# Linear attention in chunks of 64 instead of 128, with the small products in two shared PSUM banks

## The chip, the core and the metric

The kernel runs on one core of a Trainium2 chip. The metric is the device time of one execution in microseconds. A core has a matrix engine (TensorE, "PE" in the profile; its weight loads are listed as "PEld"), a vector engine (VectorE, "DVE"), a scalar engine for activations and copies (ScalarE, "ACT"), a general one (GpSimd, "POOL") and a queue for transfers (SyncE, "SP"). Each engine works through its own list of instructions in order; semaphores hold an instruction until those of other engines that it needs are done. TensorE writes its results to PSUM, which has eight banks of 512 fp32 values in each of 128 partitions; VectorE and ScalarE read them there.

## The reference

One block of a transformer in fp32: 4 sequences of 2048 tokens, 256 features. First linear attention with a running state over 16 heads of 16 features, then a mixture of 8 experts of which each token takes two, both behind a layer norm that is scaled and shifted per sequence.

```python
mod = (silu(c) @ wmod).reshape(4, 6, 1, 256)
sa, ca, ga, sb, cb, gb = (mod[:, i] for i in range(6))   # ga, gb kept away from 0
h = layernorm(x) * (1 + ca) + sa
x = x + ga * attention(h)
h = layernorm(x) * (1 + cb) + sb
x = x + gb * experts(h)

# attention: q = phi(h Wq), k = phi(h Wk), v = h Wv, phi = elu + 1, per head
S = S + k[:, None] * v[None, :]        # token by token
z = z + k
out = (S^T q) / max(z . q, 1e-6)       # then times w_out

# experts: top 2 of softmax(h w_router), at most 1280 tokens per expert in token order;
# y = sum over the two of gate * (silu(h w_gate) @ w_down[e])
```

## The kernel before

The 8192 tokens are 16 groups of 512 (`G`), a group is four steps of 128 tokens, and a sequence is four groups. A program of two halves: the attention half (to about 605 us of the span) goes through the 64 steps, and writes the rows of the expert stage to a DRAM array by indirect transfers; the expert half reads them in blocks and adds its results to the output.

In the attention half the order of TensorE, ScalarE, VectorE and GpSimd is the order in which the code names the instructions. While step `s` (group `g`, step `j` of it, counted from 0) attends, the same loop works on other groups: the queries, keys, values and denominators of group `g + 1` (`nxt`), the layer norm and keys of `g + 2` (`nrm`), the row sums of `g + 3` (`far`), the second norm, router logits and ranks of `g - 1` (`prv`), the slots and the sending of rows of `g - 2` (`old`). `early` is group 14, `tail` group 15 and the closing step.

Attention over a chunk of 128 tokens, for all heads at once in strips of 32 partitions (`a`) and two halves (`h`):

- `scores` (L494) multiplies keys and queries into `psc`, 4 banks, and VectorE masks them to the causal triangle in two instructions (L500) into `at`.
- `from_state` (L557) multiplies the state before the chunk with the scaled queries `qs` into the bank `po`; `attend` (L570) adds the masked scores times the values. `from_state` of a step is issued at the end of its turn, `attend` in the next turn.
- `keep_state` (L514) multiplies the chunk's keys and values into other columns of `po`. `take_out` (L525) copies both out on ScalarE; GpSimd adds the new part to the state and masks it (L538, L540).
- `project_out` (L588) multiplies the result with the output weights into a bank `pw`; VectorE adds it to the residual `x` (L589) and takes its statistics (L325).

Around it, per group: `project` (L375; `exk`, `exq` and relu on ScalarE, L379 and L380; the final product on VectorE, L384 and L389), `running_keys` (scan L433 on VectorE, product `qs` L438 on GpSimd), `denominators` (`pd` L446, `den` L451, `rden` L453), `scaled_q` (`pr` L464, `qs` L471), `heads_apart` (`qeo` L484 on ScalarE), `keys_by_token` (transposes L417), `values` (L397, copied to `vpad` L405), `sums`, squares in `deviations` and `normalise` (ScalarE, L282, L309, L348), `to_features` (L361, `hTa` and `hTm` L362). The router: `logits` (`pl` L640, `lgT` L645), `logits_by_token` (`lt` L653), `ranks` (L669 to L699, with one exp on ScalarE, L672), `positions` (`pp` L707 and L708, `pos` L712), `dispatch` (13 small products and an integer cast on VectorE, L731 to L753), `scale_rows` (GpSimd, L612), `shift_rows` (VectorE, L618), `send` (L770, the indirect transfers on GpSimd's queue).

PSUM: three banks `ps` that turn over among all products (`bank`), four for `psc`, one for `po`. The framework orders accesses of different engines to the same tile in PSUM by semaphores.

Of the kernel before, what the change touches and what calls it, by code (L numbers as in the profile page):

```python
# [40 lines left out]
P = 128  # L42
# [7 lines left out]
NT = G // P  # L50
GPB = L // G
# [7 lines left out]
SLOTS = NE * CAP  # L59
O_GB, O_CW, O_TOK, W = D, 2 * D, 2 * D + NE, 2 * D + NE + 4  # L60
# [7 lines left out]
def adaln_block(ctx: ExitStack, tc, x, wqkvT, woutT, wrT, wgT, wdT, cT, wmod, out):  # L68
# [4 lines left out]
    ps = ctx.enter_context(tc.tile_pool(name="ps", bufs=3, space=PSUM))  # L73
# [16 lines left out]
    tri = const.tile([P, P], F32, name="tri")  # L90
    bd = const.tile([P, 2, DH], F32, name="bd")
# [24 lines left out]
    ps_o = tokens.enter_context(tc.tile_pool(name="ps_o", bufs=1, space=PSUM))  # L116
    w1 = tokens.enter_context(tc.tile_pool(name="w1", bufs=1))
# [35 lines left out]
    def constants_last():  # L153
        make_upper_triangular(nc, tri, 1.0, diag=True)
        nc.gpsimd.tensor_copy(bd, par.unsqueeze(2).to_broadcast([P, 2, DH]))
# [61 lines left out]
    def row_products(i, pair):  # L217
        pg = bank(f"pg_{i}")
        for n, m in enumerate(pair):
            for k in range(NH):  # L220
                nc.tensor.matmul(
                    pg[:NB, n * D : (n + 1) * D], sc[:, k, :], wmod_sb[:, k, m * D : (m + 1) * D],
                    start=(k == 0), stop=(k == NH - 1),
                )
        return pg
# [71 lines left out]

    def deviations(m, a):

        nm = G_.pop("nm")  # L300
# [4 lines left out]
        if a is not None:  # L305
            xn = G_["xna", a]
            sq = small.tile([P, NT], F32, tag="sqa", name=f"sqa_{a}")
            for j in range(NT):
                nc.scalar.activation(  # L309
                    xn[:, j, :], xs[a][:, j, :], AF.Square, bias=nm[:, NT + j : NT + j + 1],  # L310
                    accum_out=sq[:, j : j + 1],
                )
            nc.gpsimd.tensor_scalar(ve[:, NT:], sq, 1.0 / D, LN_EPS, ALU.mult, ALU.add)
# [126 lines left out]
    def denominators(g):  # L440

        zq = G_["qs", g]
        pd = bank(f"pd_{g}")
        for h in range(NH):
            for j in range(NT):
                nc.tensor.matmul(  # L446
                    pd[32 * j : 32 * j + 32, :P], hpick[:, h, :], zq[:, h, j * P : (j + 1) * P],
# [3 lines left out]
        nc.vector.tensor_scalar(den, pd[:, :P], DEN_EPS, None, ALU.max)  # L451
# [5 lines left out]
    def scaled_q(g):  # L457
# [3 lines left out]
        pr = ps_sc.tile([P, 4, NH, 2, P], F32, tag="psc", name=f"pr_{g}")  # L461
        for h in range(NH):
            for j in range(NT):
                nc.tensor.matmul(  # L464
                    pr[:, j, h, 0, :],
# [4 lines left out]
        for h in range(NH):  # L470
            nc.vector.tensor_tensor(  # L471
                qs[:, h, :].rearrange("p (j t) -> p j t", t=P), qT[:, h, :].rearrange("p (j t) -> p j t", t=P),
                pr[:, :, h, 0, :], ALU.mult,
# [13 lines left out]
    def scores(g, j):  # L487
        kT, qeo = G_["k", g], G_["qeo", g]
        cols = slice(j * P, (j + 1) * P)
        psc = ps_sc.tile([P, 4, NH, 2, P], F32, tag="psc", name=f"psc_{g}_{j}")  # L490
        for h in range(NH):
            for a in range(4):
                r = 32 * a
                nc.tensor.matmul(  # L494
                    psc[:, a, h], kT[r : r + 32, h, cols], qeo[r : r + 32, h, :, cols],
                    start=True, stop=True,
                )
        for m in range(2):
            at = w4.tile([P, 2 * NH * 2, P], F32, tag="at", name=f"at_{g}_{j}_{m}")
            masked = nc.vector.tensor_tensor(  # L500
                at,
                psc[:, 2 * m : 2 * m + 2].rearrange("p i h q t -> p (i h q) t"),
                tri.unsqueeze(1).to_broadcast([P, 2 * NH * 2, P]),
                ALU.mult,
            )
            G_["at", g, j, m] = at.rearrange("p (i h q) t -> p i h q t", i=2, h=NH)
        return masked

    def keep_state(g, j):

        both, vp = G_["po"], vpads[g % 2]
        for h in range(NH):
            for a in range(4):
                nc.tensor.matmul(  # L514
                    both[32 * a : 32 * a + 32, D + 32 * h : D + 32 * h + 32],
                    G_["kk", g][:, j, h, 32 * a : 32 * a + 32], vp[:, j, h * 4 + a, 0::2, :],
                    start=True, stop=True,
                )

    def take_out(last, g, j):  # L520

        lo = 0 if last is not None else D
        hi = D + 32 * NH if g is not None else D
        both = w2.tile([P, D + 32 * NH], F32, tag="both", name=f"both_{g}_{j}")
        nc.scalar.copy(both[:, lo:hi], G_["po"][:, lo:hi])  # L525
        if last is not None:
            G_[("oT",) + last] = both[:, :D].rearrange("p (h t) -> p h t", h=NH)
        if g is None:
            return
        add = both[:, D:]  # L530
        if g % GPB == 0 and j == 0:
            G_["s_acc"] = add
        elif g % GPB == 0 and j == 1:
            s_acc = w1.tile([P, NH * 32], F32, tag="s_acc", name=f"s_acc_{g}")
            nc.gpsimd.tensor_tensor(s_acc, G_["s_acc"], add, ALU.add)
            G_["s_acc"] = s_acc
        else:
            nc.gpsimd.tensor_tensor(G_["s_acc"], G_["s_acc"], add, ALU.add)  # L538
        s_msk = w2.tile([P, NH, 2, DH], F32, tag="s_msk", name=f"s_msk_{g}_{j}")
        nc.gpsimd.tensor_tensor(  # L540
            s_msk, G_["s_acc"].rearrange("p (h q e) -> p h q e", h=NH, q=2),
# [599 lines left out]
```

## Time and profile before

| | before |
|---|---|
| median of 9 runs | 913.71 us |
| lowest, highest | 910.29, 918.58 us |
| the profiled execution, time | 917.34 us |
| its span, first to last instruction | 915.4 us |
| mean granted TensorE clock | 0.957 |
| busy: PE, DVE, ACT, POOL | 826.9, 567.9, 419.0, 476.7 us |
| scores, masks (L494, L500) | 74.5 us of 1024 records, 150.1 us of 128 |
| attend, from state, keep (L570, L557, L514) | 69.9, 40.8, 18.1 us |

The durations below come from this one profiled execution. The profile counts a TensorE instruction twice (an fp32 matmul is two records of 2 x 128 columns and the like), and records that run side by side in different strips overlap, so that busy time and mean durations of the narrow products say little; from the start of one block to the start of the next is what they cost. An "idle before" in brackets names the engine and line whose end ended the wait.

### The profile page before, as it was taken

To read this page: it belongs to the slowest core of one execution; us is meant where nothing else is said; L and a number is where in the kernel's file an instruction comes from. 1 tells how busy PE (TensorE), PEld (TensorE's weight loads), DVE (VectorE), ACT (ScalarE), POOL (GpSimd) and SP (SyncE) were. 2 spreads that over 40 slices of the span, in tenths; PEclk is the share of its full clock that TensorE was granted. 3 is DMA by queue.
4 is the path that set the end of the run, shared out by engine and by line. 5 is a ranking of instruction groups with operands and counts; after the bars stand their busy time and mean duration, and the time that the engine had idled before them with its cause. 6 is when DMAs were issued, how large, how long until landed. Compare 5 with 4: busy or idle time off the path is not lost.

```text
span 915.4 us, 20612 instructions
## 1 busy us (share of the span) xinstructions
PE 826.9 (90%) x8245; PEld 577.5 (63%) x8245; DVE 567.9 (62%) x1158; ACT 419.0 (46%) x972; POOL 476.7 (52%) x605
## 2 busy tenths in 40 slices
PE   6899989999999899999999977539999999999995
PEld 3476657657567567667657655336776767767764
DVE  3666788988888888988888885513333333333331
ACT  3557757666566566576667413212222222222220
POOL 2333356675576576576667576523443444434334
PEclk9999999999999999999999988659999999999998
DMA  8399862342442242232122111155665656545233
GB/s 291 112 360 347 214 138 70 106 141 68 120 137 97 75 142 88 95 111 86 52 76 63 41 53 35 58 200 140 146 140 106 133 109 148 109 102 111 35 34 41
DMA packets 75111, 108.25 MB, mean 118 GB/s; under 512 B 9578, under 2 KB 47218, under 8 KB 75016
## 3 DMA queue, kind: packets, MB, share of 16 engines
q1 hardware_dynamic: 47672, 68.91, 24.7%
q0 software_dynamic: 21760, 31.99, 16.1%
q10 hardware_dynamic: 5584, 6.04, 2.0%
q8 instruction: 65, 1.06, 0.5%
q14 instruction: 30, 0.25, 0.1%
HBM read 45.07 MB, written 74.69 MB: 131 GB/s over the span
## 4 chain that ended last, share of the span: by engine, by line
PE 66%; DVE 15%; issue 6%; POOL 5%; ACT 4%; DMA 2%; POOLq 0%; DVEq 0%; ACTq 0%; SPq 0%
PE ph L821 14%; PE pe L834 13%; PE pq L375 6%; PE pv L397 5%; PE psc L494 5%; PE pk L375 5%; PE po L570 5%; PE pw L588 4%; DVE at L500 3%; PE po L557 3%; DVE sel L751 2%; DVE qs L471 2%; POOL slots L770 2%; PE pte L810 2%; ACT hrow L348 2%
## 5 line engine op out<-in xcount | busy, mean ns | idle before, releaser
L843 POOL DMA_INDIRECT out_dram<-y,tok x80 | 123.3, 1541 | 180.8 <-DVE y L839 126.8
L500 DVE TENSOR_TENSOR at<-psc,tri 128x1024 f32<-128x1024 f32 x128 | 150.1, 1214 | 30.2 <-PE psc L494 29.9
L770 POOL DMA_INDIRECT slots<-hrow,idx x128 | 129.2, 1009 | 53.8 <-issue 38.7
L821 PE MATMUL ph<-hTe,wg_sb 128*128 128x512 f32 (+1 forms) x384 | 153.5, 527 | 0.0
L834 PE MATMUL pe<-wd,hid 128*128 128x256 f32 x640 | 150.5, 379 | 0.0
L827 DVE SCALAR_TENSOR_TENSOR hid<-th,ph 128x512 f32<-128x512 f32 (+1 forms) x96 | 57.5, 599 | 146.4 <-ACT th L826 146.4
L834 PEld LDWEIGHTS pe<-wd,hid 128*128 128x128 f32 x640 | 121.6, 190 | 37.0 <-issue 23.0
L826 ACT ACTIVATE th<-ph 128x512 f32<-128x512 f32 (+1 forms) x96 | 50.5, 526 | 156.4 <-PE ph L821 156.4
L821 PEld LDWEIGHTS ph<-hTe,wg_sb 128*128 128x128 f32 x384 | 70.3, 193 | 39.0 <-issue 32.5
L375 PE MATMUL pk<-hTa,wqkv_sb 128*128 128x512 f32 x128 | 70.4, 680 | 22.8 <-DVE gates L671 22.7
L494 PE MATMUL psc<-qeo,k 32*128 32x256 f32 x1024 | 74.5, 405 | 2.4 <-DVE qs L471 1.0
L588 PE MATMUL pw<-wob,both 128*128 128x256 f32 x236 | 63.3, 391 | 7.8 <-ACT both L525 5.5
L570 PE MATMUL po<-at,vpad 128*32 128x128 f32 x2048 | 69.9, 278 | 0.0
L839 DVE SCALAR_TENSOR_TENSOR y<-pe,rows 128x256 f32<-128x256 f32 x80 | 38.7, 484 | 49.6 <-PE pe L834 49.6
L570 PEld LDWEIGHTS po<-at,vpad 128*32 128x32 f32 x2048 | 53.9, 111 | 17.1 <-issue 17.0
L375 PE MATMUL pq<-hTa,wqkv_sb 128*128 128x512 f32 x128 | 61.3, 603 | 0.0
L494 PEld LDWEIGHTS psc<-qeo,k 32*128 32x128 f32 x1024 | 47.7, 187 | 19.7 <-issue 13.4
L397 PE MATMUL pv<-wqkv_sb,hTa 128*128 128x256 f32 x256 | 59.2, 384 | 0.0
L588 PEld LDWEIGHTS pw<-wob,both 128*128 128x128 f32 x236 | 41.8, 192 | 25.1 <-issue 10.1
L813 ACT COPY hTe<-pte 128x512 f32<-128x512 f32 (+1 forms) x48 | 24.7, 514 | 70.9 <-PE pte L810 70.8
L375 PEld LDWEIGHTS pk<-hTa,wqkv_sb 128*128 128x128 f32 x128 | 23.8, 203 | 47.6 <-issue 46.0
L397 PEld LDWEIGHTS pv<-wqkv_sb,hTa 128*128 128x128 f32 x256 | 47.6, 190 | 6.5 <-issue 0.4
(166 smaller groups left out, 1351.6 us busy)
## 6 DMA issues: line engine op xcount, KB each, us to landing
slots<-free SPq DMA_DIRECT2D x80, 262.0 KB, 4.9
rows<-slots SPq DMA_DIRECT2D x16, 1048.0 KB, 6.3
x<-in_x_dram SPq DMA_DIRECT2D x16, 512.0 KB, 5.9
out_dram<-x SPq DMA_DIRECT2D x16, 512.0 KB, 2.9
hrow<-mod_d SPq DMA_DIRECT2D x48, 128.0 KB, 3.6
rows<-slots SPq DMA_DIRECT2D x8, 524.0 KB, 4.6
wd<-in_wdT_dram ACTq DMA_DIRECT2D x8, 512.0 KB, 4.7
slots<-hrow,idx POOLq DMA_INDIRECT x128, 2.9
```

The lines of the kernel that those rows point to most:

```text
L375: nc.tensor.matmul(pq, wqkv_sb[:, k, o + h * P : o + (h + 1) * P], hT[:, k, :], start=(k == 0), stop=(k == NH - 1))
L397: nc.tensor.matmul(pv[:, i * D : (i + 1) * D], hT[:, k, (j + i) * P : (j + i + 1) * P], wqkv_sb[:, k, 2 * D : 3 * D], start=(k == 0), stop ...
L494: nc.tensor.matmul(psc[:, a, h], kT[r : r + 32, h, cols], qeo[r : r + 32, h, :, cols], start=True, stop=True,)
L500: masked = nc.vector.tensor_tensor(at, psc[:, 2 * m : 2 * m + 2].rearrange("p i h q t -> p (i h q) t"), tri.unsqueeze(1).to_broadcast([P, ...
L570: nc.tensor.matmul(po[32 * a : 32 * a + 32, h * P : (h + 1) * P], vp[:, j, h * 4 + a, q : q + 2, :], att[a // 2][:, a % 2, h, q, :], start ...
L588: nc.tensor.matmul(pw[:, :D], oT[:, h, :], wob[:, h, :], start=(h == 0), stop=(h == NH - 1))
L770: row = nc.gpsimd.indirect_dma_start(out=slots[:, :], out_offset=bass.IndirectOffsetOnAxis(ap=idx[:, c, j : j + 1], axis=0), in_=hr[:, j0 ...
L821: nc.tensor.matmul(ph[:, :m], wg_sb[:, k, f * P : (f + 1) * P], hTs[b][:, k, :m], start=(k == 0), stop=(k == NH - 1),)
L826: nc.scalar.activation(th[:, :m], ph[:, :m], AF.Tanh, scale=0.5)
L827: nc.vector.scalar_tensor_tensor(hids[b][:, f, :m], th[:, :m], 1.0, ph[:, :m], ALU.add, ALU.mult)
L834: nc.tensor.matmul(pe[:, :D], hids[b][:, f, j * P : (j + 1) * P], wds[e][:, f, :], start=(f == 0), stop=(f == NF - 1),)
L843: put = nc.gpsimd.indirect_dma_start(out=out[:, :], out_offset=bass.IndirectOffsetOnAxis(ap=toks[b][:, j : j + 1], axis=0), in_=y, in_offs ...
```

## The change

Attention works on two chunks of 64 tokens within a step. `scores` computes the two 64x64 diagonal blocks instead of one of 128x128, and one mask instruction covers all four strips. `po` is now one tile of two banks, allocated once, bank `c` for chunk `c`; the state is carried over twice per step, so `from_state` is issued for chunk 0 at the end of the turn and for chunk 1 in the next turn, ahead of `attend`. `take_out` copies the result on ScalarE; the new state is masked by VectorE straight out of PSUM (`new`) and added by GpSimd. The small products `pd`, `pw`, `pl`, `lt`, `pp` and `pg` move to free columns of `po`, and `ps` shrinks to two banks, which hold projections, transposes and values and are read by ScalarE (in the last group and the setup some small ones stay there). The order around it changes: squares and sums are issued ahead of `take_out`, the second norm too; `shift_rows` moves from step 1 to step 0, `dispatch` from step 2 to step 1, `send` of a group begins in step 2 instead of step 3.

```diff
-    ps = ctx.enter_context(tc.tile_pool(name="ps", bufs=3, space=PSUM))
+    ps = ctx.enter_context(tc.tile_pool(name="ps", bufs=2, space=PSUM))
...
+    po = ps_o.tile([P, 2, 512], F32, tag="po", name="po")
...
+    def squares(a):
+        xn, nm = G_["xna", a], G_["nm"]
+        sq = G_["sq", a] = small.tile([P, NT], F32, tag="sqa", name=f"sqa_{a}")
+        for j in range(NT):
+            nc.scalar.activation(
+                xn[:, j, :], xs[a][:, j, :], AF.Square, bias=nm[:, NT + j : NT + j + 1],
+                accum_out=sq[:, j : j + 1],
+            )
...
-        pd = bank(f"pd_{g}")
+        pd = po[:, 0, O_SMALL : O_SMALL + P]
...
     def scores(g, j):
+        psc = ps_sc.tile([P, 4, 512], F32, tag="psc", name=f"psc_{g}_{j}")
+        hq = psc[:, :, : NH * 2 * C].rearrange("p a (h q t) -> p a h q t", h=NH, q=2)
+        for h in range(NH):
+            for c in range(2):
+                cols = slice(j * P + c * C, j * P + (c + 1) * C)
+                for a in range(4):
+                    r = 32 * a
+                    nc.tensor.matmul(
+                        hq[c * C : (c + 1) * C, a, h], kT[r : r + 32, h, cols], qeo[r : r + 32, h, :, cols],
+                        start=True, stop=True,
+                    )
+        at = w4.tile([P, 4, NH * 2, C], F32, tag="at", name=f"at_{g}_{j}")
+        masked = nc.vector.tensor_tensor(
+            at,
+            psc[:, :, : NH * 2 * C].rearrange("p a (n t) -> p a n t", t=C),
+            tri_c.unsqueeze(1).unsqueeze(1).to_broadcast([P, 4, NH * 2, C]),
+            ALU.mult,
+        )
...
+    def keep_state(g, j, cs):
+        vp = vpads[g % 2]
         for h in range(NH):
             for a in range(4):
+                for c in cs:
+                    rows_ = slice(c * C, (c + 1) * C)
+                    o = NH * C + h * 32
+                    nc.tensor.matmul(
+                        po[32 * a : 32 * a + 32, c, o : o + 32],
+                        G_["kk", g][rows_, j, h, 32 * a : 32 * a + 32], vp[rows_, j, h * 4 + a, 0::2, :],
+                        start=True, stop=True,
+                    )
+
+    def take_out(last, g, j, cs):
+        n, o, k = NH * 32, NH * C, len(cs)
         if last is not None:
+            oT = G_[("oT",) + last] = w2.tile([P, NH, 2, C], F32, tag="oT", name=f"oT_{g}_{j}")
+            nc.scalar.copy(
+                oT.rearrange("p h c t -> p c h t"), po[:, :, :o].rearrange("p c (h t) -> p c h t", t=C)
+            )
...
+        st = w2.tile([P, 2, n], F32, tag="st", name=f"st_{g}_{j}", bufs=3)
+        new = st if first else w2.tile([P, 2, n], F32, tag="new", name=f"new_{g}_{j}")
+        nc.vector.tensor_tensor(
+            new[:, :k].rearrange("p c (h q e) -> p c h q e", h=NH, q=2),
+            po[:, :k, o : o + n].rearrange("p c (h q e) -> p c h q e", h=NH, q=2),
+            bd.unsqueeze(1).unsqueeze(1).to_broadcast([P, k, NH, 2, DH]), ALU.mult,
+        )
+        if not first:
+            nc.gpsimd.tensor_tensor(st[:, 0], G_["state"], new[:, 0], ALU.add)
+        if k == 2:
+            nc.gpsimd.tensor_tensor(st[:, 1], st[:, 0], new[:, 1], ALU.add)
...
     def project_out(g, j):
-        pw = bank(f"pw_{g}_{j}")
+        pw = po[:, 1, O_SMALL : O_SMALL + D]
...
-    def logits_by_token(part):
+    def logits_by_token(part, beside=False):
-        lt = G_["lt", part] = bank(f"lt_{g}_{j0}")
+        lt = G_["lt", part] = po[:, 0, O_SMALL : O_SMALL + P] if beside else bank(f"lt_{g}_{j0}")
...
+            if prv is not None and j == 2 and not early:
+                second_norm(prv)
+            if not tail and j == 0 and s > 0 and nrm is not None:
+                squares(nrm)
+            if not tail and j == 3 and far is not None:
+                sums(far)
             if last is not None:
+                from_state(*last, 1)
                 attend(*last)
...
+            keep_state(g, j, cs)
+            if prv is not None and j == (2 if early else 3):
+                logits(prv, beside=True)
+            if old is not None and j == 1:
+                positions(old, beside=True)
+            take_out(last, g, j, cs)
...
-            if old is not None and j == 3 and not early:
-                send(old, 0, 3)
+            if old is not None and j in (2, 3) and not early:
+                send(old, 3 * (j - 2), 3 * (j - 1))
...
             if g < NG:
-                from_state(g, j)
-                G_["s_old"] = G_.get("s_new")
+                from_state(g, j, 0)
+                G_["state"] = G_["next"]
```

`from_state` and `attend` change in the same way as `keep_state`: an inner loop over the chunks, 64 partitions and 64 columns where there were 128.

## The prediction

> **What bounds the kernel now.** I read the page's chain first: where does the time lie that set the end? Two thirds on TensorE.
>
> ```profile
> span 915.4 us, 20612 instructions
> PE 66%; DVE 15%; issue 6%; POOL 5%; ACT 4%; DMA 2%; POOLq 0%; DVEq 0%; ACTq 0%; SPq 0%
> ```
>
> The expert half (from 605 us) is not touched. The attention half is 16 groups of four steps, mostly 33 to 35 us each, so I read one steady group in the timeline (start, duration, engine, line). TensorE:
>
> ```profile
> 335.25 1.03 PE L588 MATMUL pw<-wob,both 128*128 128x256 f32 x4
> 338.18 1.96 PE L375 MATMUL pk<-hTa,wqkv_sb 128*128 128x512 f32 x4 [1.91 <-DVE gates L671]
> 340.06 0.64 PE L557 MATMUL po<-qs,s_msk 32*32 32x128 f32 x16
> 340.63 1.15 PE L494 MATMUL psc<-qeo,k 32*128 32x256 f32 x16
> ...
> 345.53 1.88 PE L375 MATMUL pq<-hTa,wqkv_sb 128*128 128x512 f32 x4
> 347.34 0.64 PE L557 MATMUL po<-qs,s_msk 32*32 32x128 f32 x16
> 347.91 1.15 PE L494 MATMUL psc<-qeo,k 32*128 32x256 f32 x16
> 348.98 1.08 PE L570 MATMUL po<-at,vpad 128*32 128x128 f32 x32
> 349.88 0.31 PE L514 MATMUL po<-vpad,kk 128*32 128x32 f32 x16
> 350.12 1.09 PE L417 MATMUL pk<-ident,k 128*128 128x128 f32 x8
> ```
>
> Start to start, a step's attention costs 0.57 (from the state) + 1.07 (scores) + 0.90 (attend) + 0.24 (keep) = 2.78 us. TensorE has one hole per group, 1.91 us before the second key projection, whose bank the router's logits hold until VectorE has read them. VectorE in the same group:
>
> ```profile
> 341.25 0.41 DVE L589 TENSOR_TENSOR x<-x,pw 128x256 f32<-128x256 f32 x1
> 348.56 0.69 DVE L384 SCALAR_TENSOR_TENSOR q<-exq,q 128x512 f32<-128x512 f32 x1 [0.77 <-ACT q L380]
> 349.17 1.28 DVE L433 TENSOR_TENSOR_SCAN zc<-ones_g,zc,k 128x512 f32<-128x512 f32 x1
> 350.37 2.33 DVE L500 TENSOR_TENSOR at<-psc,tri 128x1024 f32<-128x1024 f32 x2
> 355.04 1.27 DVE L618 TENSOR_TENSOR hrow<-hrow,modr 128x1024 f32<-128x1024 f32 x1
> 365.83 2.02 DVE L751 SCALAR_TENSOR_TENSOR sel<-rank,slot 128x32 f32<-128x32 f32 x1
> ```
>
> VectorE runs late and it costs nothing: the residual add of step 3 (341.25) ends 11 us after that step's scores began (330.67), and no TensorE work stands behind it, since its bank rotates. A 32-element product takes 2.02 us where it mostly takes 0.19: GpSimd's 2.37 us product ran from 365.43 to 367.80.
>
> Last, the granted clock in two stretches (columns after the five engines: clock, DMA share, GB/s):
>
> ```profile
> 232.00:267.00 35.00, 32.95 (x447) 22.18 (x446) 29.08 (x57) 22.00 (x54) 22.58 (x33) 0.95 0.35 119
> 335.00:368.00 33.00, 30.93 (x446) 21.81 (x445) 28.81 (x57) 21.62 (x54) 21.97 (x32) 1.00 0.34 116
> ```
>
> In the first the projection after the hole took 3.50 us instead of 1.96. In the chain it takes 3.02, 3.50, 3.41 and 3.42 in four of the twelve groups with that hole: the clock fell, at a cost of 1.4 us on average.
>
> **Part by part: the work.** A block's time is about 0.1 us of switching, a first weight load, and packs of strips that run side by side: a pack of four takes 0.109 us where 128 columns stream (eight packs in attend, four in state), 0.03 us for 32. Halved chunks double the instructions and halve the streamed columns, with twice the strips. If eight run side by side: scores 4 x 0.109 + 0.16 = 0.60; attend 8 x 0.055 + 0.13 = 0.57; state 4 x 0.055 + 0.13 = 0.35, now twice; keep 0.24 to 0.36, I take 0.30. Sum 2.17, so 0.6 us less per step, 38 us over 64 steps if TensorE set the time. If only four run side by side, scores stay at 1.03 and attend at 1.0, and a step costs 3.0: both ends are kept.
>
> VectorE drops 64 of 128 masks (1.21 us each, 78 us) and gains 64 products of 128x128 out of PSUM (row of den, 0.28 us: 18 us). ScalarE's copy goes from 320 to 256 columns; GpSimd trades a masking for a second add (0.5 us each). These count only where something waits.
>
> **The waits.** All small results now lie in the one tile po. The built program lists what each instruction waits for, and po is held whole: ScalarE's copy of oT comes before VectorE's product "new"; pw (L588's successor) waits for new, in step 2 for den, in step 3 for the read of the logits (steps counted from 0); and the next step's state products wait for the residual add. So each step makes a round trip PE, ACT, DVE, PE. I follow a group from mark to mark.
>
> *P (end of the second query projection, 347.34) to V (end of values, 355.91): 8.57 before.* VectorE is through the scan at 350.37, P + 3.03. The shift of rows has moved here (1.20), then one mask (1.13) and new (0.30): P + 5.66. TensorE reaches pw at P + 3.4 (0.35 + 0.60 + 0.35 + 0.57 + 0.30, positions 0.36, transposes 0.93). A hole of 2.3 us where there was none. V = 5.75 + pw 0.87 + values 3.63 = 10.25, so +1.7.
>
> *V to S3 (scores of step 3, 363.74): 7.83 before.* ScalarE copies vpad until V + 0.64, normalises four rows (2.0, now ahead of the oT copy), copies (0.36): V + 3.0; new until V + 3.35. Then pd 0.56, den, pw, rden 0.95, pr 0.68, transposes 1.0, qs: S3 at V + 7.55, with two holes of 0.4. That is -0.3. But the 13 small products of dispatch now stand before this step's mask, and start while GpSimd multiplies qs (1.27 us). One of them may be held, as sel was: 0 to 1.0 on this path; I take 0.5. Net +0.2.
>
> *S3 to S0 (scores of the next group, 340.63): 9.95 before.* ScalarE: hTm ends at S3 + 0.7, sums 1.6 (now ahead), lgT and oT until S3 + 3.05. Then, in its order, two qeo (1.3), exk and relu of the first keys (0.95), two qeo (1.3), and only then the exp of the gates: S3 + 6.8. From there VectorE needs 2.92 us to the residual add in the trace (338.33 to 341.25), + 0.41: S3 + 10.15. TensorE has finished both key projections at S3 + 7.7. The old hole of 1.91 goes (0.7 before pw is left); a hole of 2.5 before the state products takes its place. S0 = 10.25 + 0.35 = 10.6, so +0.65.
>
> *S0 to P: 6.71 before.* The squares, moved ahead of the oT copy (4 x 0.49), end before TensorE is through its first projection, which covers them. If it did not, pw would wait up to 1 us. Only here do the narrower tiles count: 0.60 + 0.35 + 0.57 + 0.24 + 4.5 = 6.25, so -0.45.
>
> Sum: +1.7 + 0.2 + 0.65 - 0.45 = +2.1 us per group. Groups 2 to 13 are like this: 12 x 2.1 = 25. Groups 0 and 1 lack the shift or the ranks, and group 14 and the last one (502 to 605 us) wait on GpSimd's sends and small chains; there the earlier sends (3 x 1.3 us out of group 14) and shorter masks stand against the new round trips: 0, between -6 and +6.
>
> The clock: two holes of 2.3 to 2.5 us per group instead of one of 1.9. If half of them are followed by a drop of 1.4 us: 1.4 - 0.33 x 1.4 = 0.9 per group, 11 us; bounds 0 and 12 x 2.3 = 28. [...]
>
> 25 + 11 = 36 on the profiled 917.3 us (span 915.4 and 1.9 around it). That execution is 3.6 us over the median of 913.7, so on the median: **950 us**.
>
> **The rivals.**
> - Faster: TensorE stays the bound, because the round trips end in time. Then each group loses 4 x 0.6 and the 1.9 us hole: 4.3 x 13 = 56 us, 858 us. For it: the single hole of now, and VectorE losing 60 us of work. Against it: P + 5.66 is the finish of instructions that stand in this order. It decides if new ends by P + 3.4 and the residual add by S3 + 7.7.
> - Slower, but no more clock drops: 913.7 + 25 = 939. For it, eight of twelve holes without a drop.
> - Narrow strips do not run side by side: 0.85 us more per step on the path in three of the four stretches, 2.4 per group, 29 us: 979. For side by side: the four of a pack start 7 ns apart in all forms of now. Eight are not shown.
> - The strips and the waits cancel: within 3 us of 914.
>
> **Numbers.** Forecast 0.60; no clock drops 0.16; strips 0.09; cancel 0.03; faster 0.12. A difference within 0.3% (2.7 us) can't be told from none. Slower 0.60 + 0.16 + 0.09 = 0.85, same 0.03, faster 0.12. Low end: 913.7 + 25 - 12 (half of each group's 2.1, if durations are shorter) - 6 = 920. High end: 25 + 28 + 6 = 59, and part of the strips' rival: 978.
>
> **What would show it.** Right: TensorE idle before pw in step 1 and before the first state product at the end of step 3, each over 2 us, put down to VectorE; groups of 35 to 37 us; attention's four blocks shorter, 2.1 to 2.3 us per step; granted clock below 1.00 in most groups; masks halved to 78 us. Wrong: groups under 31 us, or holes under 1 us at those two places; or scores still at 1.0 us, which is the strips' rival.

## The result, and the profile after

The changed kernel takes 1014.4 us (median of 20 runs, 1006 to 1033), the kernel before 914.0 in the runs beside it: ratio 1.108, 95% interval [1.105, 1.110]. Slower, as forecast, but by 100 us where 36 were forecast and 64 was the end of the range.

The profiled execution of the changed kernel took 1035 us, 2% over its median; sums from it are on the high side, and single holes and blocks are as in the others. Its page:

```profile
span 1033.4 us, 30905 instructions
...
q8 instruction: 105, 1.72, 0.7%
...
PE 61%; DVE 15%; issue 11%; ACT 5%; POOL 3%; DMA 2%; POOLq 0%; DVEq 0%; SPq 0%; ACTq 0%
```

The page of before has this for the same queue:

```profile
q8 instruction: 65, 1.06, 0.5%
```

Two things stand out: "issue", time in which an engine waits for nothing that the profile shows, has gone from 6% to 11% of the chain; and the queue that carries instructions moved 105 packets of 16 KB instead of 65. TensorE's waits (total us, times, longest) say where:

```profile
PE po L570 <- POOL cnt L713: 31.4, 13, 2.6
PE po L530 <- issue: 26.1, 10, 9.9
PE po L602 <- DVE new L550: 21.1, 12, 3.3
PE po L585 <- issue: 19.0, 10, 4.0
```

The first and third are the two holes that the prediction named: the state product at the end of step 3 (its releaser is named by the instruction that ended last; in the built program it waits for the residual addition L603), and the output projection pw in step 1. The second and fourth were in no step of the prediction: they stand *inside* a block, between two instructions of the same line. The timeline of TensorE shows all of them within one group and the start of the next:

```profile
376.61 1.07 PE L429 MATMUL pk<-ident,k 128*128 128x128 f32 x8
379.82 1.10 PE L602 MATMUL po<-wob,oT 128*128 128x256 f32 x4 [2.14 <-DVE new L550]
...
398.25 1.13 PE L602 MATMUL po<-wob,oT 128*128 128x256 f32 x4 [0.51 <-DVE gates L685]
399.22 1.88 PE L387 MATMUL pk<-hTa,wqkv_sb 128*128 128x512 f32 x4
403.61 0.42 PE L570 MATMUL po<-qs,st 32*32 32x64 f32 x16 [2.50 <-POOL cnt L713]
...
407.75 0.34 PE L530 MATMUL po<-vpad,kk 64*32 64x32 f32 x9 [1.52 <-issue]
408.01 3.78 PE L387 MATMUL pq<-hTa,wqkv_sb 128*128 128x512 f32 x4
...
412.77 1.88 PE L387 MATMUL pq<-hTa,wqkv_sb 128*128 128x512 f32 x4
...
415.91 0.68 PE L585 MATMUL po<-at,vpad 64*32 64x64 f32 x43
418.08 0.36 PE L585 MATMUL po<-at,vpad 64*32 64x64 f32 x19 [1.50 <-issue]
...
419.33 1.95 PE L429 MATMUL pk<-ident,k 128*128 128x128 f32 x8
```

The holes cost the clock as well. By the trace's record of the granted clock it stands at 0.50 from 405.40 to 412.22 us, behind the 2.50 us hole and across the one of 1.52: the first query projection takes 3.78 us, the second, 5 us later, 1.88. It is at 0.50 again from 419.05 to 422.46, behind the 1.50 us hole: the eight transposes (L429) take 1.95 us instead of 1.07.

What ends the holes inside blocks is read from the trace's records of DMA packets on the instruction queue:

| packet starts | has landed | hole inside a block | TensorE goes on after the landing |
|---|---|---|---|
| 366.79 | 368.10 | 367.68 to 369.36 | 1.26 us |
| 405.12 | 406.32 | 406.23 to 407.75 | 1.43 |
| 415.18 | 416.81 | 416.59 to 418.08 | 1.28 |
| 437.78 | 438.85 | 436.33 to 440.30 | 1.45 |
| 485.45 | 486.49 | 485.73 to 487.81 | 1.33 |

TensorE's 13365 matmul and 13365 weight load records make 255 for each of the 105 packets; in the kernel before 2 x 8245 make 254 for each of 65. So a packet is the next 256 instructions of TensorE. The order of the trace confirms it: with the 166 semaphore instructions that it lists for TensorE there are 26896, 105 times 256 and 16 over, and all 23 "issue" holes of over 0.3 us in the attention half end at the 194th or 195th instruction after a multiple of 256. The same count gives the same two places for all 112 such holes in runs 2, 3, 4, 5, 8 and 11 below, whichever product stands there. TensorE goes on 1.1 to 1.6 us after the landing in all 135.

Two packets are never closer than 3.2 us, seldom than 3.4, in any trace with 104 packets or more (4.7 us in the kernel before), and attention now uses 320 records per step (matmuls and weight loads) in 2.4 us, where it used 160 in 2.8.

### The profile page after: what moved, and what is told of

The parts are those of the page before. It is cut to its first block, busy times and chain, and to the rows that moved or that the text cites. A ratio compares the mean times of both kernels' runs of the same rounds, so it can differ in the third digit from the quotient of the medians.

```text
span 1033.4 us, 30905 instructions
## 1 busy us (share of the span) xinstructions
PE 855.0 (83%) x13365; PEld 596.0 (58%) x13365; DVE 499.6 (48%) x1158; ACT 415.4 (40%) x971; POOL 466.6 (45%) x611
## 4 chain that ended last, share of the span: by engine, by line
PE 61%; DVE 15%; issue 11%; ACT 5%; POOL 3%; DMA 2%; POOLq 0%; DVEq 0%; SPq 0%; ACTq 0%
PE ph L835 12%; PE pe L848 12%; PE pq L387 6%; PE po L602 5%; PE po L585 4%; PE pk L387 4%; PE psc L508 3%; PE po L570 3%; PE pv L409 3%; DVE qs L483 2%; PE pte L824 2%; PE po L530 2%; DVE at L513 2%; ACT qeo L496 2%; DVE zc L445 2%
## 5 line engine op out<-in xcount | busy, mean ns | idle before, releaser
L602 PE MATMUL po<-wob,oT 128*128 128x256 f32 x256 | 79.8, 439 | 34.3 <-DVE new L550 21.1
L513 DVE TENSOR_TENSOR at<-psc,tri_c 128x1024 f32<-128x1024 f32 x64 | 77.9, 1218 | 25.1 <-PE psc L508 25.1
L602 PEld LDWEIGHTS po<-wob,oT 128*128 128x128 f32 x256 | 50.9, 215 | 65.1 <-DVE new L550 16.7
L570 PE MATMUL po<-qs,st 32*32 32x64 f32 x1984 | 54.9, 226 | 34.4 <-POOL cnt L713 31.4
L585 PE MATMUL po<-at,vpad 64*32 64x64 f32 x4096 | 64.2, 240 | 19.5 <-issue 19.0
L570 PEld LDWEIGHTS po<-qs,st 32*32 32x32 f32 x1984 | 34.6, 107 | 74.2 <-POOL cnt L713 44.0
L556 POOL TENSOR_TENSOR st<-st,new 128x64 f32<-128x64 f32 x60 | 19.1, 318 | 121.0 <-DVE new L550 120.1
L450 POOL TENSOR_TENSOR qs<-zc,q 128x512 f32<-128x512 f32 x32 | 43.4, 1357 | 53.1 <-DVE slot L745 40.0
L585 PEld LDWEIGHTS po<-at,vpad 64*32 64x32 f32 x4096 | 49.4, 113 | 29.0 <-issue 23.7
L530 PE MATMUL po<-vpad,kk 64*32 64x32 f32 x1984 | 38.5, 211 | 26.2 <-issue 26.1
```

Of the source, the lines that this page charges most:

```text
L513: masked = nc.vector.tensor_tensor(at, psc[:, :, : NH * 2 * C].rearrange("p a (n t) -> p a n t", t=C), tri_c.unsqueeze(1).unsqueeze(1).to_ ...
L530: nc.tensor.matmul(po[32 * a : 32 * a + 32, c, o : o + 32], G_["kk", g][rows_, j, h, 32 * a : 32 * a + 32], vp[rows_, j, h * 4 + a, 0::2, ...
L570: nc.tensor.matmul(po[r, c, h * C : (h + 1) * C], st[r, h * 32 : (h + 1) * 32], G_["qs", g][r, h, j * P + c * C : j * P + (c + 1) * C], st ...
L585: nc.tensor.matmul(po[32 * a : 32 * a + 32, c, h * C : (h + 1) * C], vp[rows_, j, h * 4 + a, q : q + 2, :], att[rows_, a, h, q, :], start= ...
L602: nc.tensor.matmul(pw, oT[:, h].rearrange("p c t -> p (c t)"), wob[:, h, :], start=(h == 0), stop=(h == NH - 1))
```

## The experiments

Theory F, formed on the above: TensorE uses its instructions up faster than the packets bring them. Rival W: all of the loss is round trips through the shared tile, and clock. A "hole inside a block" is an "issue" hole, nearly always between two instructions of one block; "undisturbed" means without one and at full clock. Where no other is named, the kernel before took 912 to 916 us beside a run.

**1. Order and banks without the halved chunks.** The changed kernel's order, banks and waits, chunks of 128:

```diff
-C = P // 2
+C = P          # one chunk per step: one from_state, two masks, one addition to the state
```

> The changed kernel with its order, its shared banks and its waits, but with attention in chunks of 128 again: 16 records of from_state, 16 of scores, 32 of attend, 16 of keep per step instead of twice as many, two masks again, one addition to the state. Theory F (TensorE's instructions: they arrive 256 records of matmul and weight load at a time, one packet of 16 KB of the instruction queue, and a step's attention now uses more than that in 2.5 us, faster than the next packet comes): some 65 packets of that queue instead of 105, no TensorE hole in the middle of a block that only 'issue' explains, where the changed kernel has about 20 with 48 us in sum; the two holes of 2 us per group behind VectorE stay. Against the changed kernel's 1014 us: -48, + 0.4 x 64 = 25 for the wider blocks, + about 12 for the second mask ahead of the first step's round trip: some 1000 us, 980 to 1010. Theory W (all of the loss is round trips through the shared tile, and the holes inside blocks are what a trace shows when the clock is low): the round trips are at least as long, since VectorE has 78 us more, and nothing is won back: 1014 + 25 + 12, 1035 to 1060 us.

1020.3 us, ratio 1.115 [1.110, 1.120], 65 packets, and no hole inside a block, as F had it; the time lies between the two ranges. The run parts the change in two: the order and the banks alone cost 104 us, and halving the chunks then gives 6 back. Groups 2 to 13 tell why 6: they take 41.1 us on average, and in the changed kernel, its holes inside blocks taken off, 37.9 (run 5) and 38.2 (run 11). That is 3 us per group, some 40 for 13 groups, and the holes cost 34 to 48 us again. The round trips and the clock are read here without the rest. Waits, then windows with TensorE's busy time, granted clock, DMA share, GB/s, for the scores after the 2.5 us hole and those of the next step:

```profile
PE po L595 <- DVE new L548: 42.9, 18, 3.0
PE po L565 <- POOL cnt L706: 32.5, 13, 2.5
```

```profile
402.32:404.41 2.09, 2.09 (x24) 0.51 0.10 30
410.54:411.69 1.15, 1.15 (x24) 1.00 0.87 313
```

The same 1.15 us block takes 2.09 at clock 0.51.

**2. The number of instructions alone.** The kernel before, each attention product cut in two by columns (scores, from_state and keep likewise):

```diff
+                    for c in range(0, P, P // 2):
-                        po[32 * a : 32 * a + 32, h * P : (h + 1) * P], vp[...],
-                        att[a // 2][:, a % 2, h, q, :],
+                        po[32 * a : 32 * a + 32, h * P + c : h * P + c + P // 2], vp[...],
+                        att[a // 2][:, a % 2, h, q, c : c + P // 2],
```

> The kernel before, its order, banks and chunks of 128 untouched, but each of attention's matmuls is cut in two along its streamed columns (scores 2 x 128 instead of 256, attend and from_state 2 x 64 instead of 128, keep 2 x 16 instead of 32). The result is the same and so are the streamed columns; TensorE has as many instructions as in the changed kernel. Theory F: some 105 packets on the instruction queue, and TensorE holes of 1 to 4 us inside attention's blocks that end 1.3 to 1.5 us after such a packet has landed; 40 to 60 us slower, 950 to 975 us, with drops of the granted clock behind the holes. Theory W: the number of instructions costs nothing by itself; a cut pack is no longer than the uncut one, or by its weight loads at most 0.3 us per step: 914 to 934 us, and no holes inside blocks.

951.9 us, ratio 1.039 [1.034, 1.045], 104 packets. The holes inside blocks are there, in a kernel that shares nothing and waits for nothing new:

```profile
398.65 0.34 PE L516 MATMUL po<-vpad,kk 128*32 128x16 f32 x18
401.37 0.32 PE L516 MATMUL po<-vpad,kk 128*32 128x16 f32 x11 [2.37 <-issue]
```

The packet of that hole landed at 400.03, 1.34 us before its end. The profiled run is 41 us longer than that of before; 23 us are such holes, the rest is mostly the cut packs' own time (from the start of step 0 to the end of the second query projection 7.19 us instead of 6.77). F holds. W fails as the whole account: cutting the products in two, with nothing else changed, costs 36 us.

**3. and 4. The two named holes taken out of the changed kernel.** Run 4 has the second edit alone:

```diff
@@ step 0 @@
-                if old is not None:
-                    shift_rows(old)
@@ step 1, ahead of dispatch(old) @@
+                    shift_rows(old)
@@ step 3 @@
+                done()
                 if prv is not None and not early:
                     logits_by_token(prv, beside=True)
                     ranks(prv)
-                done()
```

> The changed kernel with the two round trips taken apart that the prediction named: the shift of rows goes from step 0 back to step 1 (ahead of dispatch), so that VectorE is free earlier for 'new' in step 1; and in step 3 the output projection pw and its residual addition stand ahead of the router's transposed logits and ranks, so that the next state product no longer waits for the chain of the ranks. Theory W: the holes before pw in step 1 (1.7 to 2.1 us) and before the first state product (2.4 us) go, 0.5 us is left of each: 12 x 3.3 = 40 us and some clock, 960 to 978 us. Theory F: the same two holes go, 40 us, and the holes inside blocks stay, with 105 packets: 965 to 985 us, still far above 914. If these two holes are covered anyway (what is next late takes their place): 1005 to 1020 us.

> The changed kernel with only the second of those two edits: in step 3 the output projection and its residual addition ahead of the transposed logits and the ranks. By the prediction's account the 2.4 us hole before the state product goes in 13 groups and 0.3 to 0.7 us is left of it: 25 us less than the changed kernel, and about 5 for the clock: 980 to 995 us. If the 2.4 us only move (the transposed logits now wait for the residual addition, and the second key projection stands behind them): 1005 to 1020 us.

988.1 us (1.082 [1.076, 1.087]) and 984.2 us (1.076 [1.071, 1.081]). Run 3 lies just above the ranges of both theories. The second edit gives 30 us, as said: 0.5 us is left of the 2.5, before the transposed logits, and the state product follows at once (run 4):

```profile
233.67 0.33 PE L667 MATMUL po<-ident,lgT 128*128 128x128 f32 x1 [0.51 <-DVE x L603]
233.84 1.88 PE L387 MATMUL pk<-hTa,wqkv_sb 128*128 128x512 f32 x4
235.65 0.43 PE L570 MATMUL po<-qs,st 32*32 32x64 f32 x16
```

The first edit gives nothing: undisturbed, the stretch that ends with the values goes from 10.13 to 8.99 us, and the next one from 8.65 to 9.56, where the denominators now wait 1.6 us for "new". The shift of rows costs VectorE 1.2 us wherever it stands ahead of such a read. In both the holes inside blocks stay, with 105 packets.

**5. What makes one of those holes 10 us long.** The changed kernel's longest is 9.9 us, at 107 us.

```diff
-                if 4 + s < TPE:
-                    free_slots(4 + s, masked)
```

> The changed kernel without the fills of the free slots that it issues in steps 0 to 5 (48 transfers of 262 KB; the first 32 of the setup stay): its output lacks the marks in those slots, everything else is as it was. In the changed kernel the longest hole inside a block is 9.9 us, at 107 us, in a stretch where only these fills move (some 80 packets of 1 KB per us at 160 to 200 ns each, against 45 to 60 ns elsewhere), and the packet of instructions starts 7 us after the hole has begun. If such a packet queues behind bulk transfers: the hole of 8 to 10 us in group 1 shrinks to the 1 to 3 us of the others, 7 to 10 us less: about 1005 us. If the packet is late for another reason (its request comes late): the hole stays, 1012 to 1016 us.

1012.0 us, no less: by time alone this is what was expected if the packet's request comes late. The hole in group 1 fell to 1.6 us, but one of 9.1 us stood in group 0. What had moved with it is another transfer, the rows that second_norm spreads over all partitions (SyncE, then TensorE):

```profile
60.74 12.75 SPq L616 DMA_DIRECT2D hrow<-mod_d  x12
```

```profile
75.41 0.43 PE L530 MATMUL po<-vpad,kk 64*32 64x32 f32 x23 [9.10 <-issue]
```

In the changed kernel they stand behind the fills, issued from 101 to 115 us, the hole lies at 107 to 117; in run 2 they are issued until 115 us and their packets move until 124, and the hole of 8.6 us lies at 119 to 128. In all three the instruction packet starts 6.1 to 7.4 us after the hole has begun, while these packets take 150 to 210 ns each instead of 45 to 60, or (run 5) some 80 of them per us move. That the packet queues behind them fits all three; but in run 3 it started 2.1 us after the hole had begun (a hole of 4.5 us) while the same transfers moved, and no run took them away. Why these packets are late is not shown.

**6. and 7. The kernel before without its own hole.** Run 6 only moves the second key projection ahead of the transposed logits; run 7 takes from the change only the place of those logits, in free columns of attention's bank:

```diff
-        lt = G_["lt", part] = bank(f"lt_{g}_{j0}")
+        lt = G_["lt", part] = G_["po"][:, 320:448] if beside else bank(f"lt_{g}_{j0}")
```

> The kernel before with one move: in step 3 the second key projection stands ahead of the router's transposed logits and ranks, so that it takes a bank that ScalarE has already read and no longer the one that holds the logits until VectorE has read them. Everything else, chunks of 128 too, as before. If TensorE sets the time around that hole: 12 holes of 1.9 us go (23 us) and with them the clock drops that follow four of them (6 us): 880 to 893 us. If the wait moves (the residual addition of step 3 comes 2 us later, and the next group's projections wait for its bank): 905 to 914 us.

> The kernel before with the one part of the change that answers its own hole: the transposed logits of step 3 lie in free columns of the bank that holds attention's result, so that the second key projection finds a bank; the next state product, 2 us later, waits for VectorE's read instead. The read ends at about the time at which the projection is through, so 0 to 0.3 us is left of the 1.9 us: 882 to 895 us. If VectorE's read comes later without the projection's wait ahead of it, the hole moves to the state product: 905 to 914 us.

888.2 us (0.969 [0.964, 0.975]) and 884.7 us (0.965 [0.960, 0.971]), each in the range expected: both beat both kernels. TensorE goes without a hole from the first key projection to the next group (run 7), groups take 30.9 us instead of 33 to 35, and the time by which blocks exceed their fast duration falls from 17 to 11 us:

```profile
351.37 0.27 PE L653 MATMUL po<-ident,lgT 128*128 128x128 f32 x1
351.48 1.03 PE L588 MATMUL pw<-wob,both 128*128 128x256 f32 x4
352.35 1.88 PE L375 MATMUL pk<-hTa,wqkv_sb 128*128 128x512 f32 x4
354.16 0.64 PE L557 MATMUL po<-qs,s_msk 32*32 32x128 f32 x16
```

**8. The same instructions, spread out.** Run 4's kernel, in step 0 the two query projections moved between attention's blocks:

```diff
+            if not tail and j == 0:
+                project(nxt, "q", 0, 0, 1)      # after scores, was after keep
             if last is not None:
                 from_state(*last, 1)
...
-                done()
                 project(nxt, "q", 1, 0, 1)
+                done()
```

> The changed kernel with the output projection of step 3 ahead of the ranks (as in the kernel that took the hole before the state product out, 984 us) and, in step 0, the same TensorE instructions in another order: the first query projection stands between scores and the rest of attention's blocks, the second one between keep and the output projection. No instruction more or less. Theory F: step 0 had 160 records in 2.4 us, now 48, then 4 in 2 us, then 112; the packets have time to come, and the 1.3 us of such holes per group between the start of step 0 and the end of the second query projection fall below 0.3: 12 to 18 us less than 984, 966 to 975 us, the step's round trip being covered by the second projection besides. If the holes have to do with the number of instructions alone: as many of them, somewhere else in the group, 980 to 988 us.

967.4 us, 1.052 [1.044, 1.061], 17 us under run 4. Holes inside blocks from the start of step 0 to the second query projection: 0.26 us per group instead of 1.28, with as many packets. So the number of instructions alone does not make the holes; how close they stand does. Some 4 of the 17 us are another gain: the second projection now covers the 0.33 us for which pw of step 0 waited, and a quiet group is 0.3 us shorter by it.

**9., 12., 13., 14. One tile or two.** Run 1's kernel with attention's result in one tile and the small products in another (only as wide as chunks of 128 leave room for):

```diff
-    po = ps_o.tile([P, 2, 512], F32, tag="po", name="po")
+    po = ps_o.tile([P, 1, 512], F32, tag="po", name="po")
+    pm = ps_o.tile([P, 512], F32, tag="pm", name="pm")
-        pw = po[:, 1, O_PW : O_PW + D]          # pd, pl, lt, pp likewise
+        pw = pm[:, :D]
```

> The kernel with the changed order and banks but chunks of 128 (1020 us), with its two shared banks taken as two tiles instead of one: attention's result and the state's new part in the one, the six small products (pw, pd, logits, transposed logits, positions, setup rows) in the other. The order of every engine stays. The output projection then no longer waits for VectorE's 'new', nor the state product for the residual addition. If the loss of that kernel comes from results and small products being one tile: its holes before the output projection (41 us in the attention half) and before the state product (32 us) go for the most part, 60 us or more, 935 to 965 us. If it comes from the order alone (VectorE is late with the residual addition, and the next small product waits for that in the second tile as well): the holes are renamed and stay, 995 to 1020 us.

> The kernel with two tiles (929 us) with the setup's gate rows in a projection bank, as in the kernel before, and no longer in the second tile, where the first denominators overwrote them before they were read; the 64 steps are untouched. If the 929 us are those of the shared banks taken apart, the time stays: 925 to 935 us. If wrong gate rows changed what the experts get and so the time: anything else.

> The two-tile kernel with the setup rows in a projection bank, once more, beside the one-tile kernel of the next run. If the tile is the cause: 85 to 95 us less than the one-tile kernel, 925 to 935 us where the kernel before takes 914; a ratio to before of about 1.02. If what ran before was the overwritten rows' doing: less than 60 us below the one-tile kernel.

> The kernel with the changed order and banks, one tile, chunks of 128, once more: 1015 to 1025 us where the kernel before takes 914, a ratio of 1.11 to 1.12, whichever theory holds.

In run 9 the setup's gate rows also lie in the second tile, where the first denominators overwrite them before they are read, so that its experts work with wrong rows; runs 12 and 13 keep them in a projection bank. Run 9: 929.3 us, ratio 1.019 [1.014, 1.024], 91 us less than run 1, more than the 60 expected. Runs 12 to 14 fell on chips where the kernel before itself takes 963 us (below): 945.8 and 943.9 us with two tiles (run 13: 0.984 [0.978, 0.989]), 1026.8 with one (1.068 [1.062, 1.074]). The ranges expected of runs 12 to 14 were for a kernel before of 914 us and fail with it; the difference side by side, 83 us, is just under the 85 to 95 expected. It is the price of one tile instead of two. Which bank some small products lie in changes with it (pd, pl, lt and pp stand beside attention's result in the one, apart from it in the other), and no run separates the two. The overwritten rows of run 9 made no difference that shows. The two holes are gone (run 13; pw of step 1 behind the transposes, the state product behind the projection):

```profile
295.10 1.07 PE L428 MATMUL pk<-ident,k 128*128 128x128 f32 x8
296.01 1.03 PE L596 MATMUL pm<-wob,oT 128*128 128x256 f32 x4
...
317.54 1.88 PE L386 MATMUL pk<-hTa,wqkv_sb 128*128 128x512 f32 x4
319.35 0.64 PE L566 MATMUL po<-qs,st 32*32 32x128 f32 x16
```

The order's part is what is left, 17 us in run 9: there pw of step 2 waits 2.4 us for the denominators, because dispatch now stands ahead of the masks. On the chips of runs 12 and 13 the same kernel is 17 and 19 us faster than the one before, so this part has no sign that holds on both.

**10. A smaller cut.** Run 2 with only scores and from_state cut, 112 matmul records per step instead of 160 (80 before):

> The kernel before with only scores and from_state cut in two along their streamed columns; attend and keep as before. A step's attention has 112 records where the kernel before has 80 and the fully cut one 160; the smallest distance between two packets of instructions in any trace so far is 3.3 us for 128 records. Theory F: 112 records take about 2.9 us, which is near that rate, so few holes are left: at most 8 us of them instead of 41 us, some 90 packets, and a block cost of 0.1 to 0.2 us per step: 920 to 932 us. If a product cut in two costs time whatever the rate of instructions: half of the fully cut kernel's 36 us, 932 to 940 us, without holes.

919.5 us, 1.007 [1.005, 1.010], half a microsecond under F's range, 80 packets where some 90 were expected, and 4.5 us of "issue" holes in all; undisturbed groups take 33.7 us instead of 33.0, which with these holes more than covers the 7 us. (The 41 us in the text above is run 2's whole difference; its holes were 23.) Where the packets keep up, cutting these products in two costs 0.1 to 0.2 us per step.

**11., 15., 16. The kernels once more.**

> The changed kernel itself once more, for a profile to set beside the others. 1006 to 1020 us; the holes before the state product (about 2.4 us each) and before the output projection of step 1 (about 1.7 us), and holes inside attention's blocks that end 1.3 to 1.5 us after a packet of instructions has landed, in about the same places of the program as in the first profile.

1026.3 us, one run; 46 us of holes inside blocks, in the same places as far as the groups can be told apart, the longest 9.3 us at the same point of group 1. Run 1's 1020 less 40 for the narrower blocks plus these 46 is 1026. That this comes out to the microsecond is luck: the 40 was taken in part from this run, and the same sum gives 1014 for the profiled execution of run 5, which took 1007, and 1028 for the first one, which took 1035.

> The kernel before itself, for a profile. On a chip like the first: 909 to 919 us, one hole of 1.9 us per group before the second key projection and 33 to 35 us per group. On the chip where it took 963: 45 us more in the attention half; if it is the wait for the logits that grows, that hole is 4 to 5 us in 12 groups.

> The kernel before with the transposed logits in free columns of attention's bank, once more (885 us beside 916). On a chip like the first: a ratio of 0.96 to 0.97. On the one where the kernel before took 963: if the wait for the logits is what grew there, 885 to 900 us, a ratio of 0.92 to 0.935; if something else grew that this kernel has too, 925 to 935 us.

960.9 us for the kernel before, 935.4 for run 7's, ratio 0.973 [0.970, 0.976], which is the reading that something else grew, in both kernels. The 45 us more do lie in the attention half, but not in the wait for the logits: the hole before the second key projection is as it was (23.8 us in all), and from the values to step 3 a group takes 10.9 us instead of 7.9, in the short kernel as well. The 16 records of the denominators, 0.62 us before, are drawn out while GpSimd issues the indirect transfers:

```profile
379.42 0.41 PE L446 MATMUL pd<-qs,hpick 128*32 128x128 f32 x4 [0.23 <-issue]
380.15 0.43 PE L446 MATMUL pd<-qs,hpick 128*32 128x128 f32 x6 [0.31 <-issue]
380.87 0.43 PE L446 MATMUL pd<-qs,hpick 128*32 128x128 f32 x3 [0.30 <-issue]
```

Why some chips do this stays open. It bears on the comparison of runs 12 to 16 with the others only, and each of those is read beside its own neighbours.

## Why the prediction was right, and where it was wrong

*The mechanism of the waits: right.* "po is held whole", and each step makes a round trip: runs 13 and 14 show it, 83 us between one tile and two. The two holes stand where they were put and are about as long as given: 2.14 us in the group shown, elsewhere mostly 1.7 or 2.1, against 2.3 before pw of step 1, 2.5 against 2.5 before the state product.

*The marks.* In undisturbed groups P to V was forecast at 10.25 us and takes 10.13; S3 to the next S0 10.6 and 10.92; V to S3 8.03 and 8.65; S0 to P 6.25 and 7.12 (run 4, where no slow clock reaches into it). So a quiet group takes 36.8 us, not 35.15. The last of these failed mostly for two reasons: blocks cost 2.38 us per step (keep 0.40 instead of 0.30, and attend 0.65 instead of 0.57) where 2.17 were taken, and pw of step 0 waits 0.3 us. That eight strips run side by side was right (in attend the eight records of a pack start 5 to 8 ns apart); the rival that they don't is out.

*The step that failed: "Halved chunks double the instructions", costed at nothing.* The prediction went on to streamed columns and strips; that instructions have to arrive was in no term and no rival. What the runs showed in its place: 34 to 48 us of holes that end with the landing of an instruction packet. In the profiled run the attention half is 117 us longer (the expert half is the same to 0.6 us): 48 us are holes ended by instruction packets; 35 us are blocks longer than the fast ones of their kind (53 instead of 17; each block against the tenth percentile of its kind, differences over 0.15 us); 34 us are left for waits less the gain of narrower blocks, where the sum had 25. In run 5's shorter execution the same three are 34, 19 and 37.

*The clock: right in kind, too small.* The forecast was 11 us, from half of two holes per group at 1.4 us. (The chain of before has five slow projections in the twelve groups, not four: the one at 470.26 us took 2.93. That moves the 11 by less than 1.) Measured 19 to 35 us, by the lengths of blocks; half of the time in which TensorE worked at half clock gives 25 to 41. In run 1, which has only the two holes, the slow blocks sum to 51 us instead of 17, slow scores behind the state product's hole in all 12 groups; and the holes inside blocks add their own.

When a hole costs the clock, the trace's record of it shows. In all 18 profiles the granted clock is 1.00 or 0.50 and changes only on a grid of 3.41 us. In the attention halves each of the 113 grid steps at full clock in which no matmul ran for 2.0 us or more is followed by a step at half; of 2107 steps with less than 1.5 us of such time 14 are; in between, 89 of 180. From half clock the next step is full in 150 of 159 cases with under 0.4 us, and in 1 of 68 with 0.6 us or more. So what counts in these traces is how much of a hole falls into one grid step. Of the twelve holes ahead of the second key projection in the kernel before, six lay wholly in one step (1.88 to 2.18 us) and five of them were followed by a step at half; of the six that the edge of a step divided (at most 1.71 us in one) none was. That "half of them" would be was a guess. The groups of run 1, 41.0 us, are almost exactly twelve grid steps long, which puts its hole into the same place of a step again and again.

*The sum by parts.* Order and banks +104 (83 to 91 of it between one tile and two), narrower blocks and the single mask -40, late instructions with +34 to +48. The forecast's +36 stands for the first two, which come to +64: a quiet group is 1.7 us longer than forecast, 20 us in twelve, and the clock costs at least 8 more. The third was missing. The +64 is just the end of the stated range: without the third the time would have been there.

The packets could have been foreseen: the page of before already listed 65 packets of 16 KB on the instruction queue beside 16490 records of TensorE, 254 for each packet, and the 160 records that the change adds per step, 10240 in 64 steps, make 40 more at 256 each.

## What to carry to other kernels

Cutting matmuls smaller is paid in instructions (36 us in run 2). Count the matmul and weight load records of the densest stretch and divide by its time. Where 256 of them take less than about 3.4 us, the usual least distance of two packets here, expect holes that the profile calls "issue" and a clock that drops behind them; the steps that had many used 320 records in 2.4 to 3.2 us, and run 10, with 224 in 3.0, is just at that rate and had 4.5 us of them. Put long matmuls between the dense blocks (17 us here) before giving up the cut. Give products that different engines read at different times different tiles: the six small products in the tile of attention's result cost 83 us against a tile of their own. Before a rebuild, look whether one wait can be taken away by itself: one product in another bank gave 31 us.

## What was not expected of the hardware

- TensorE's instructions came in packets of 16 KB, 256 instructions each, here at most one in 3.2 us. All 135 holes they left, in seven profiles, end at the 194th or 195th instruction after a multiple of 256, and TensorE went on 1.1 to 1.6 us after the landing.
- Such a packet was late at times: holes of 8.6, 9.1, 9.3, 9.7 and 9.9 us (runs 2, 5, 11 and 4, and the changed kernel); in runs 2 and 5 and the changed kernel packets of the 12 transfers that spread rows from DRAM to all partitions were moving meanwhile. Why is not shown.
- The granted clock changed on a grid of 3.41 us in all 18 profiles and fell to a half after every step with 2.0 us or more without a matmul (113 of 113), after 1.5 to 2.0 us in 89 of 180: a block of 1.15 us then took 2.09 (run 1).
- The same kernel took 914 us on some chips and 961 on others, 3 us per group of it in one stretch of step 2 (10.9 us instead of 7.9, run 15).
